# Sixteen blocks of a conditioned transformer layer: the attention's projection ahead of the last part of the MLP and of v

## The chip, the cores and the metric

The kernel runs on one core of one Trainium2 chip. A core has a matrix engine (TensorE, in the profile PE), a vector engine (DVE), a scalar engine (ACT), a general one (POOL) and a queue that issues DMAs (SP). Time is the device time of one execution in microseconds; of several executions the median is given.

## The reference

Everything is 32-bit floating point. For each of eight sequences of 1024 tokens of width 512, with a condition vector of its own, the layer computes:

```python
mod = jax.nn.silu(condition) @ Wada + bada
sh_a, sc_a, gt_a, sh_m, sc_m, gt_m = jnp.split(mod, 6, axis=1)
xm = layernorm(x) * (1.0 + sc_a) + sh_a
x = x + gt_a * attention(xm)           # 16 heads of 32, causal, softmax, then @ Wproj + bproj
xm = layernorm(x) * (1.0 + sc_m) + sh_m
h = jax.nn.gelu(xm @ W1 + b1)          # 512 -> 2048
x = x + gt_m * (h @ W2 + b2)           # 2048 -> 512
```

(the normalizations also have gains and offsets of their own; the modulation is a row for each sequence).

## The kernel before, in words

**Blocks and steps.** The 8 x 1024 tokens are cut into 16 blocks of 512 tokens, two a sequence: an even block is the first half of its sequence, an odd one the second half. A block goes through these steps, which are names in the plan: `at` (its normalized input is brought into the transposed layout and modulated), `q`, `k`, `v` (three projections), the attention in four groups of four heads, `proj` (the attention's output times Wproj, gated and added to the residual, and the second normalization set going), `mt` (the transposed, modulated input of the MLP; its 16 transposes are the matmuls of L735 that read `hat_m`), `u` 0 to 3 (the four quarters of the first MLP matrix) and `d` 0 to 3 (four parts of the second).

**Products in seven.** `q`, `k`, `v`, `u` and `d` use Strassen's scheme: seven products of half size in place of eight, on sums of weight pieces and of inputs that are kept. A `q`, `k`, `v` or `u` step is 7 products of 32 matmul instructions. `d` has 7 products of 128: two in `d0`, two in `d1`, one in `d2`, two in `d3`. In `d2` DVE combines its product into `u_d`, and three element-wise operations (POOL or DVE, as the planner finds them free) settle `v_d` into the residual `xr`. `proj` is 4 row tiles of 4 channel groups of 8 matmul instructions (N = 512), 128 in all. All of them are issued by one helper, line 202.

**Two streams on one engine.** TensorE runs two streams, interleaved: the attention (scores L1541, transposed weights L1620 and L1632, weighted values L1672, sums L1693, rows of maxima L1594), and the linear work, which is the list `plan`, sixteen windows in a row, one for each block w of the attention. Window w has the rest of the MLP of block w - 2, v of block w, `proj` and `mt` of block n = w - 1, k and q of block w + 1, and the first parts of the MLP of block n. A planner written in Python fixes the order of all instructions when the program is built, with estimated durations: the linear stream is paced so that window w ends when the attention of block w does (`stream["due"]` against `done_linear`). When linear work is behind, it goes first; when it is ahead, the attention goes first and the linear work fills its waits. Each engine then runs its own instructions in that order, and waits for others by semaphores where data or buffers ask for it.

**What orders the steps.** The main thread takes the steps of the plan strictly one after the other; `at`, `mt`, loads of the residual and stores are side threads, which run when what they ask for is there. A step asks by keys with times in `written`; a key at `NEVER` blocks until something sets it. `proj` of n asks for `("attended", n)`, set when the last quotient of its attention has been queued: after the sums of a group of heads, ACT copies them, DVE takes reciprocals (L1711) in four pieces, and POOL multiplies (L1736, `qT<-top,rec`). `mt` of n asks for `("v done", n + 1)`. The attention can't weigh values of block w before v of w is done (`close`, L1822): until then only linear work is issued. In an even block that is so from its first unit on; in an odd block the units over the first half of the sequence come before it. The steps of a turned `at` (blocks from 2 on): four DVE transposes, a write of 1 MB to DRAM (`held`), four reads back into the tile `hat`, four scalings. There is one `hat` tile, used by the inputs of `at` and then by those of `mt` (`hat_m`).

**Weights.** Pieces of 256 KB come through a ring of eight slots, in the order of the plan: a piece is fetched when the one eight before it has been released. `q`, `k`, `v` and `u` have seven pieces, `d0`, `d1` and `d3` eight, `d2` four, `proj` four, which are all released at its end. SP issues all of these DMAs, and the loads of inputs, the stores and the turns, in one order.

Of the kernel before, what the change touches and what calls it, by code (L numbers as in the profile page):

```python
# [22 lines left out]
def kernel(  # L23
# [42 lines left out]
    NC = D // P  # L66
# [28 lines left out]
    written, left = {}, {}  # L95
    shape = [None]
    pool_spans = []
    NEVER = float("inf")
# [13 lines left out]
    def note(engine, ns, reads=(), writes=(), port=False):  # L112
        start = max(now[engine], due(reads, writes))
        if port:
            start = max([start] + [b for a, b in pool_spans if a <= start < b])
        end = start + ns
        now[engine] = end
        if engine == "POOL":
            pool_spans.append((start, end))
            del pool_spans[:-16]  # L120
        for k in reads:
            left[k] = max(left.get(k, 0.0), end + SYNC)
        for k in writes:
            written[k] = end + SYNC
        return end
# [102 lines left out]
    def mlp_steps(n):  # L228
        return [("u", n, i) for i in range(NQ)] + [("d", n, part) for part in range(4)]
# [8 lines left out]
    late = []  # L238
    for w in range(1, NB):
        n = w - 1  # L240
        m = mlp_steps(n)
        even = blocks[n][1] == 0
        rows_a = [("rows", blocks[n][0], "a")] if even else []
        rows_m = [("rows", blocks[n][0], "m")] if even else []
        own = m[:1] + ([("load_xa", w + 2)] if w + 2 < NB else []) + m[1:3]
        own += [("norm_a", w + 2)] if w + 2 < NB else []
        if w == NB - 1:
            steps = late[:1] + rows_a + [("proj", n), ("mt", n)] + late[1:]
            steps += [("v", w)] + rows_m + own + m[3:5] + [("load_xr", w)] + m[5:6]
            late = m[6:]  # L250
        else:

            steps = late + [("v", w)] + rows_a + [("proj", n), ("mt", n), ("k", w + 1)]
            if w == 2:
                steps = late + [("v", w), ("k", w + 1)] + rows_a + [("proj", n), ("mt", n)]
            if w == 1:
                steps = rows_a + [("k", w + 1), ("proj", n), ("mt", n)]
            steps += [("q", w + 1)] + rows_m + own
            at = [("at", w + 2)] if w + 2 < NB else []
            if blocks[w][1] == 0:  # L260

                steps += m[3:5] + [("load_xr", w)]
                late = m[5:6] + at + m[6:]
            else:
                steps += m[3:5] + [("load_xr", w)] + m[5:6] + at
                late = m[6:]
        plan[w] = steps
    n = NB - 1
# [99 lines left out]
    at, r0 = [], 0  # L368
# [9 lines left out]
    def hat_tile(key):  # L378
        return tmp.tile([P, NTT, D], F32, tag="hat", name=f"hat_{key}", bufs=1)

    def load_x(n):
        b, h = blocks[n]
        rows = hat_tile(f"a{n}")
        for t in range(NTT):
            some = x[b, h * TB + t * P : h * TB + (t + 1) * P, :]
            if f"a{n}" in by_pe:
                nc.sync.dma_start(rows[:, t, :], some)
            else:
                nc.sync.dma_start(rows[ts(t, Q), :, :], some.rearrange("(t i) d -> i t d", i=Q))
        return rows  # L390
# [145 lines left out]
    act_jobs = []  # L536
# [43 lines left out]
    def normalize(tiles, key, sources):  # L580

        for t in range(NTT):
            written["hat", key, t] = NEVER
        mv = small.tile([P, NTT, 2], F32, tag="mv", name=f"mv_{key}")
        rstd = small.tile([P, NTT], F32, tag="rstd", name=f"rstd_{key}")
        offset = small.tile([P, NTT], F32, tag="offset", name=f"offset_{key}")

        def statistics(t):
            st = small.tile([P, nc.vector.BN_STATS_DIM], F32, tag="st", name=f"st_{key}_{t}")
            nc.vector.bn_stats(st, tiles[:, t, :])  # L590
            nc.vector.bn_aggr(mv[:, t, :], st)
            note("DVE", 850, [sources[t]], [("mv", key)])
            if t < NTT - 1:
                return
            if alone[0]:
                root()
                for i in range(NTT):
                    apply_tile(i)
                return
            power()  # L600
            for i in range(NTT):
                act_jobs.append((lambda i=i: apply_tile(i), [("rstd", key)]))

        def root():
            nc.scalar.activation(rstd, mv[:, :, 1], AF.Sqrt, bias=eps)
            note_act(300, "sqrt", [("mv", key)], [("rstd", key)])
            nc.vector.reciprocal(rstd, rstd)
            nc.vector.scalar_tensor_tensor(offset, mv[:, :, 0], -1.0, rstd, ALU.mult, ALU.mult)
            note("DVE", 360, [("rstd", key)], [("rstd", key)], port=True)

        def power():
            nc.gpsimd.tensor_scalar(rstd, mv[:, :, 1], EPS, None, ALU.add)
            nc.gpsimd.tensor_tensor(rstd, rstd, minus_half, ALU.pow)
            nc.gpsimd.tensor_scalar(offset, mv[:, :, 0], -1.0, None, ALU.mult)
            nc.gpsimd.tensor_tensor(offset, offset, rstd, ALU.mult)
            note("POOL", 1500, [("mv", key)], [("rstd", key)])

        to = [None]

        def apply_tile(t):  # L620
            if t == 0:
                hats[key] = to[0] = hat_tile(key) if key[0] == "m" else tiles
            xh, xt = to[0][:, t, :], tiles[:, t, :]
            reads, writes = [("rstd", key)], [("hat", key, t)]
            if (key == "a0" and t % 2) if alone[0] else sooner(reads, writes, 700, 800) == "DVE":
                nc.vector.tensor_scalar(
                    xh, xt, rstd[:, t : t + 1], offset[:, t : t + 1], ALU.mult, ALU.add
                )
                note("DVE", 700, reads, writes, port=True)
            else:  # L630
                nc.scalar.activation(
                    xh, xt, AF.Identity, bias=offset[:, t : t + 1], scale=rstd[:, t : t + 1]
                )
                note_act(800, None, reads, writes)

        for t in range(NTT):
            add_job(lambda t=t: statistics(t), [sources[t]], key[0] == "m")
# [54 lines left out]
    def modulated(key, gain, shift, b, guards):  # L692
# [22 lines left out]
        at = {t: (key, t) for t in part}  # L715
        if turned:
            yield from turn(key, got, xm)
        for c in range(NC):
            if turned:
                if c:  # L720
                    yield [("turned", key)], []
                source, out = ("turned", key), xm[:, c, :].rearrange("p (a x) -> p a x", x=P)
                values = got[:, :, ts(c, P)]
                if key[0] == "m":
                    out = xm[:, c, :].rearrange("p (t a x) -> p t a x", t=2, a=NTT)
                    values = values.rearrange("p a (t x) -> p t a x", t=2)
            else:
                if c:
                    yield [("hat", key, 0)], [BANK]
                bank = lin_bank()  # L730
                source, out, values = ("l", bank), xm[:, c, :], banks[bank]
                for t in range(NTT):
                    if t:
                        yield [("hat", key, t)], []
                    nc.tensor.transpose(banks[bank][:, ts(t, P)], got[:, t, ts(c, P)], ident)  # L735
                    note_pe(TR, "whole", [("hat", key, t)], [("l", bank)])
            writes = [at["B11"], at["T1"]] if c < 2 else [at["B21"], at["B22"]]
            if sooner([source], writes, 770, 780) == "DVE":
                nc.vector.tensor_scalar(
                    out, values, gain[:, c, b : b + 1], shift[:, c, b : b + 1],  # L740
                    ALU.mult, ALU.add,
                )
                note("DVE", 770, [source], writes, port=turned)
            else:
                nc.scalar.activation(  # L745
                    out, values, AF.Identity,
                    bias=shift[:, c, b : b + 1], scale=gain[:, c, b : b + 1],
                )
                note_act(780, None, [source], writes)
            if not turned:  # L750
                live[bank] = False
            if c == 1:
                nc.vector.tensor_tensor(part["T1"], part["T1"], part["B11"], ALU.subtract)
                note("DVE", 700, [at["B11"], at["T1"]], [at["T1"]], port=True)
# [1184 lines left out]
```

## Time and profile before

| | |
|---|---|
| median of 3 runs | 3546.27 us (3541.39 to 3548.4) |
| the profiled execution's own time | 3542.2 us |
| its span, first to last instruction | 3540.5 us |
| instructions | 120499 |
| mean granted TensorE clock | 0.998 |
| weights and data read, written in DRAM | 412.99 MB, 43.06 MB |

A row of a timeline has the start in us from the span's beginning, the length in us, the engine, the line, the operation, the tiles (output<-inputs) with partitions x elements, the number of instructions merged, and in brackets the engine's idle time before it with what ended it. `32*128` is the size of a TensorE tile in rows and columns. A row of a stage gives its bounds and length, the busy time (and instructions) of each engine in it, the granted TensorE clock, the share of the DMA engines and GB/s.

### The profile page before, as it was taken

The numbers are of one execution on the slowest core, as the hardware profiler recorded it, in microseconds if no ns is written. First come the engines' busy times: TensorE is split into PE (matmuls) and PEld (weight loads), VectorE is DVE, ScalarE is ACT, GpSimd is POOL, SyncE is SP. The second block draws the span as 40 slices with busy tenths as digits, with TensorE's granted clock in tenths as the row PEclk, the third lists the DMA queues.
The fourth block names the chain that finished last, engine by engine and source line by source line (L and its number), as shares of the span: only waits on it lengthen the run. The fifth ranks groups of instructions, "written<-read, shape, count | busy, mean of one in ns | idle before, by whom it ended". The sixth has DMA issues, their size and how long they took to land.

```text
span 3540.5 us, 120499 instructions
## 1 busy us (share of the span) xinstructions
PE 3482.5 (98%) x54621; PEld 1738.0 (49%) x54621; DVE 2174.2 (61%) x2383; ACT 1190.1 (34%) x1237; POOL 2074.9 (59%) x2249
## 2 busy tenths in 40 slices
PE   8999999999999999999999999999999999999999
PEld 4444445445554555545554454544545445454445
DVE  5776675564756557565675656656566556655563
ACT  2334323352333513235232342323423234232521
POOL 2667836666376664666546675366762667526660
PEclk9999999999999999999999999999999999999999
DMA  6753434335443354524445334443344533443334
GB/s 198 245 163 103 137 117 140 111 111 156 117 148 103 110 160 117 168 85 126 142 118 159 103 115 141 124 149 107 118 132 127 156 106 119 135 126 124 100 110 140
DMA packets 319555, 465.96 MB, mean 132 GB/s; under 512 B 26300, under 2 KB 176636, under 8 KB 316996
## 3 DMA queue, kind: packets, MB, share of 16 engines
q1 hardware_dynamic: 318928, 458.22, 42.9%
q8 instruction: 430, 7.05, 0.8%
q14 instruction: 81, 0.66, 0.1%
q10 hardware_dynamic: 116, 0.03, 0.0%
HBM read 412.99 MB, written 43.06 MB: 129 GB/s over the span
## 4 chain that ended last, share of the span: by engine, by line
PE 88%; DMA 4%; DVE 3%; POOL 2%; issue 1%; ACT 1%; SPq 0%; ACTq 0%; DVEq 0%; POOLq 0%
PE bank L202 61%; PE sc L1541 8%; PE po L1672 7%; PE st L1632 7%; PE st L1620 3%; DMA w<-in_L_cond_Wproj_dram 2%; PE bank L1693 2%; PE bank L735 1%; DVE mx L1556 1%; POOL pT L1762 1%; DMA w<-in_L_cond_Wada_dram 1%; PE bank L1594 0%; POOL hT L161 0%; POOL xr L161 0%; DVE sc L1553 0%
## 5 line engine op out<-in xcount | busy, mean ns | idle before, releaser
L1762 POOL TENSOR_TENSOR pT<-pT,pT 128x256 f32<-128x256 f32 (+3 forms) x1254 | 1207.2, 998 | 347.9 <-PE po L1672 181.4
L1644 ACT ACTIVATE pT<-st 128x2048 f32<-128x2048 f32 x288 | 541.0, 1879 | 1000.5 <-PE st L1632 883.3
L202 PE MATMUL bank<-w,hT 128*32 128x256 f32 x14336 | 812.3, 380 | 1.1 <-ACT rec L1702 0.9
L1556 DVE TENSOR_REDUCE mx<-sc 128x4 f32<-128x2048 f32 (+3 forms) x384 | 666.0, 1755 | 197.7 <-PE sc L1541 191.6
L202 PEld LDWEIGHTS bank<-w,hT 128*32 128x32 f32 x14336 | 450.4, 110 | 369.2 <-issue 81.4
L202 PE MATMUL bank<-xm_m,w 128*32 128x256 f32 x8192 | 499.6, 381 | 0.0
L202 PE MATMUL bank<-t_m,w 128*32 128x256 f32 x6144 | 381.2, 380 | 0.0
L1649 POOL TENSOR_SCALAR_AFFINE_SELECT pT<-pT 128x512 f32<-128x512 f32 x256 | 168.8, 677 | 346.6 <-ACT pT L1644 344.2
L202 PEld LDWEIGHTS bank<-xm_m,w 128*32 128x32 f32 x8192 | 255.7, 110 | 224.7 <-issue 62.4
L1553 DVE TENSOR_TENSOR sc<-sc,mask 128x1024 f32<-128x1024 f32 (+1 forms) x160 | 162.9, 1018 | 319.7 <-PE sc L1541 242.5
L1541 PE MATMUL sc<-kT,qT 32*128 32x512 f32 (+3 forms) x3072 | 329.1, 520 | 1.8 <-DVE mx L1556 1.1
L1672 PE MATMUL po<-pT,v 128*32 128x512 f32 (+3 forms) x3048 | 302.9, 492 | 2.0 <-POOL pT L1649 2.0
L1632 PE MATMUL st<-qT,kT 32*128 32x512 f32 (+3 forms) x3072 | 301.0, 487 | 0.0
L202 PEld LDWEIGHTS bank<-t_m,w 128*32 128x32 f32 x6144 | 190.0, 110 | 173.3 <-issue 48.5
L202 PE MATMUL bank<-xm_a,w 128*32 128x256 f32 x3968 | 249.3, 382 | 0.0
L202 PE MATMUL bank<-w,qT 128*32 128x512 f32 x2048 | 238.2, 594 | 8.7 <-DMA w<-in_L_cond_Wproj_dram 7.2
L1711 DVE RECIPROCAL rec<-rec 128x128 f32<-128x128 f32 x256 | 225.7, 920 | 31.5 <-ACT rec L1702 31.5
L1541 PEld LDWEIGHTS sc<-kT,qT 32*128 32x128 f32 x3072 | 129.3, 183 | 179.3 <-issue 73.0
L193 DVE TENSOR_TENSOR hT<-bank,u_u 128x512 f32<-128x512 f32 x192 | 129.9, 687 | 114.1 <-PE bank L202 107.4
L202 PE MATMUL bank<-t_a,w 128*32 128x256 f32 x2944 | 188.4, 382 | 0.4 <-ACT xm_m L745 0.4
L1069 ACT ACTIVATE hT<-hT,cols 128x512 f32<-128x512 f32 x256 | 164.4, 711 | 35.5 <-DVE hT L193 35.0
L202 PEld LDWEIGHTS bank<-xm_a,w 128*32 128x32 f32 x3968 | 122.7, 110 | 105.5 <-issue 32.6
(216 smaller groups left out, 3384.6 us busy)
## 6 DMA issues: line engine op xcount, KB each, us to landing
w<-in_L_cond_W_dram SPq DMA_DIRECT2D x384, 256.0 KB
w<-kept_up_S SPq DMA_DIRECT2D x256, 256.0 KB
w<-kept_down_S SPq DMA_DIRECT2D x256, 256.0 KB
w<-kept_qkv_S SPq DMA_DIRECT2D x180, 256.0 KB
w<-in_L_cond_Wqkv_dram SPq DMA_DIRECT2D x147, 256.0 KB
hat_a<-in_x_dram SPq DMA_DIRECT2D x64, 256.0 KB
xr<-in_x_dram SPq DMA_DIRECT2D x32, 512.0 KB
w<-in_L_cond_Wproj_dram SPq DMA_DIRECT2D x64, 256.0 KB
```

Of the source, the lines that this page charges most:

```text
L193: nc.vector.tensor_tensor(out, src, other, op)
L202: nc.tensor.matmul(ps[r, :], columns, rhs, start=start, stop=stop, skip_group_check=True)
L1069: nc.scalar.activation(hT[:, i, :], hT[:, i, :], AF.Gelu, bias=cols[:, O_B1 + f : O_B1 + f + 1])
L1541: nc.tensor.matmul(sc[:, j, c0 : c0 + w], qTs[n][r, gg, ts(qt, P)], keys_of(n, kh)[r, gg, :w], start=True, stop=True, skip_group_check=True,)
L1553: nc.vector.tensor_tensor(place, place, shape_of.to_broadcast(place.shape), ALU.add)
L1556: nc.vector.tensor_reduce(maxima[n, gg][:, kh, qt, :], sc[:, :, c0 : c0 + w], axis=AX.X, op=ALU.max)
L1632: nc.tensor.matmul(st[:, j, c0 : c0 + w], kT[r, gg, ts(k % NTT, P)], qT[r, gg, TB - w :], start=False, stop=True, skip_group_check=True,)
L1644: nc.scalar.activation(pT[:, :, :used], st[:, :, :used], AF.Exp, scale=scale)
L1649: nc.gpsimd.affine_select(diagonal, diagonal, pattern=[[0, HPG], [1, P]], compare_op=ALU.is_ge, fill=0.0, base=0, channel_multiplier=-1,)
L1672: nc.tensor.matmul(po[r, TB - w :], v[:, k % NTT, g * P + j * hd : g * P + (j + 1) * hd], pT[:, j, c0 : c0 + w], start=(k == 0), stop=last ...
L1711: nc.vector.reciprocal(some, some)
L1762: nc.gpsimd.tensor_tensor(into, into, pT[:, j, c0 : c0 + w], ALU.add)
```

## The change

In windows 3 to 14 the order of the linear steps changes. Windows 1, 2 and 15 keep theirs.

- Even windows, before: `d2 d3 v proj mt k`; after: `d2 proj mt d3 v k`.
- Odd windows, before: `d1 at d2 d3 v proj mt k`; after: `at d1 d2 proj mt d3 v k`. Here `at` is that of block w + 1, and d1 to d3 are those of block w - 2.
- In odd windows the loads of the gates' row for the new sequence (`rows_a`) go with `proj`.
- A new key, `"hat free"`: set to `NEVER` when the input of an `at` is loaded into the tile `hat`, and to 0 when the last scaling of that `at` has been issued. The scalings that write `hat_m` wait for it in the planner's list. It adds no instruction.

No computation is added, removed or changed in form; the same weight pieces are loaded in the new order of the plan.

```diff
-            steps = late + [("v", w)] + rows_a + [("proj", n), ("mt", n), ("k", w + 1)]
+            steps = late[:-1] + rows_a + [("proj", n), ("mt", n)] + late[-1:] + [("v", w), ("k", w + 1)]
             if w == 2:
                 steps = late + [("v", w), ("k", w + 1)] + rows_a + [("proj", n), ("mt", n)]
...
                 steps += m[3:5] + [("load_xr", w)]
-                late = m[5:6] + at + m[6:]
+                late = at + m[5:]
...
     def load_x(n):
         b, h = blocks[n]
         rows = hat_tile(f"a{n}")
+        written["hat free"] = NEVER
...
         for t in range(NTT):
             written["hat", key, t] = NEVER
+        free = ["hat free"] if key[0] == "m" else []
...
             power()
             for i in range(NTT):
-                act_jobs.append((lambda i=i: apply_tile(i), [("rstd", key)]))
+                act_jobs.append((lambda i=i: apply_tile(i), [("rstd", key), *free]))
...
             if not turned:
                 live[bank] = False
+            if c == NC - 1 and key[0] == "a":
+                written["hat free"] = 0.0
```

## The prediction

> **What bounds the kernel now.** First the head of the page and its table of engines.
>
> ```profile
> span 3540.5 us, 120499 instructions
> PE 3482.5 (98%) x54621; PEld 1738.0 (49%) x54621; DVE 2174.2 (61%) x2383; ACT 1190.1 (34%) x1237; POOL 2074.9 (59%) x2249
> ```
>
> TensorE works in 98% of the span: 58.0 us of idling are all that a new order can win back, while each microsecond for which it makes PE wait is a microsecond of the kernel. So the second view is who PE waited for, and I cut it to 580:3000 us, the blocks that the change touches (columns: total, times, longest).
>
> ```profile
> PE bank L202 <- DMA w<-in_L_cond_Wproj_dram: 7.2, 9, 1.5
> PE st L1620 <- DVE mx L1556: 3.8, 3, 1.6
> ```
>
> The longest of these, 7.2 us, is one wait: the projection for its weights. Third, the timeline of PE where block 7 of the attention hands over to block 8 (an even block: it needs a new v at once).
>
> ```profile
> 1685.32 1.04 PE L1693 MATMUL bank<-pT,ones 128*32 128x512 f32 x8
> ...
> 1696.53 3.23 PE L202 MATMUL bank<-w,hT 128*32 128x256 f32 x56
> 1699.58 0.41 PE L1594 MATMUL bank<-ident_b,mcols 128*32 128x128 bf16 x16
> 1699.80 13.56 PE L202 MATMUL bank<-w,hT 128*32 128x256 f32 x248
> 1723.54 1.90 PE L202 MATMUL bank<-w,qT 128*32 128x512 f32 x16
> 1726.20 1.92 PE L202 MATMUL bank<-w,qT 128*32 128x512 f32 x16 [0.75 <-DMA w<-in_L_cond_Wproj_dram]
> 1731.38 1.04 PE L1672 MATMUL po<-pT,v 128*32 128x512 f32 x8
> ```
>
> At 1685.32 the sums of the last head group of block 7 are made (L1693); from 1699.80 on PE runs the MLP's last part, v and the start of the projection in one piece, because the attention can't go on (next `po` at 1731.38) before v of block 8 is done. This piece, which I call the hold, is where all moved steps lie.
>
> **The change part by part.**
>
> *The wait for Wproj goes.* The queue of weight loads (SP) shows why it exists.
>
> ```profile
> 1712.18 0.42 SPq L1118 DMA_DIRECT2D out_dram<-xr  x1
> 1712.70 3.60 SPq L685 DMA_DIRECT2D hat_a<-held_a  x4
> 1716.39 0.85 SPq L342 DMA_DIRECT2D w<-in_L_cond_Wproj_dram  x2
> 1717.34 0.39 SPq L1118 DMA_DIRECT2D out_dram<-xr  x1
> 1717.82 1.48 SPq L342 DMA_DIRECT2D w<-in_L_cond_Wproj_dram  x2
> ```
>
> Ring slots come free in order of use, eight ahead. Today the four Wproj pieces follow the pieces of v, are issued behind stores and the turn's four reads, 7 us ahead of their use, and all four are needed in the first row tile. Afterwards they follow d2's four pieces, so their slots come free in d1's second product, and all of d2 (128 matmuls, 7.0 us by the row of 248 in 13.56 us) lies between. Gain 7.2 us, all there is; the other end is 0 (another load is late instead). Next to be late would be d3's last four pieces, whose slots the projection frees only at its end; they have d3's first product, again 128 matmuls and 7.0 us, before they are needed, and the four stores and reads above are then no longer ahead of them: I take 0. The stores of d3 move behind the projection on SP, v's and k's loads stand behind them as today. In odd windows the turn's write and four reads go ahead of d1's loads; nothing but the ring's lead of eight pieces covers them, and that is what covers them now.
>
> *A new wait: the projection for the attention's last quotient.* In odd windows the projection now stands behind d1 and d2, 384 matmuls or 21 us, and the quotient is done as they begin (first row below, window 9). In even windows only d2 is ahead of it. When d2 ends, DVE makes `u_d` of its product; when the last head group is divided by its sum, POOL writes `qT` (L1736), and the projection multiplies with that. Both, behind that first row, for the even windows 4, 6, 8, 10, 12, 14:
>
> ```profile
> 1877.27 1.27 POOL L1736 TENSOR_TENSOR qT<-top,rec 128x512 f32<-128x512 f32 x1
> 830.76 1.29 POOL L1736 TENSOR_TENSOR qT<-top,rec 128x512 f32<-128x512 f32 x1
> 832.64 0.69 DVE L193 TENSOR_TENSOR u_d<-bank,p_d 128x512 f32<-128x512 f32 x1 [1.43 <-PE bank L202]
> 1266.30 0.69 DVE L193 TENSOR_TENSOR u_d<-bank,p_d 128x512 f32<-128x512 f32 x1 [1.13 <-PE bank L202]
> 1271.04 1.73 POOL L1736 TENSOR_TENSOR qT<-top,rec 128x512 f32<-128x512 f32 x1
> 1699.40 0.69 DVE L193 TENSOR_TENSOR u_d<-bank,p_d 128x512 f32<-128x512 f32 x1 [0.42 <-PE bank L202]
> 1704.14 1.73 POOL L1736 TENSOR_TENSOR qT<-top,rec 128x512 f32<-128x512 f32 x1
> 2131.80 0.69 DVE L193 TENSOR_TENSOR u_d<-bank,p_d 128x512 f32<-128x512 f32 x1 [0.38 <-PE bank L202]
> 2137.13 1.28 POOL L1736 TENSOR_TENSOR qT<-top,rec 128x512 f32<-128x512 f32 x1
> 2566.12 0.69 DVE L193 TENSOR_TENSOR u_d<-bank,p_d 128x512 f32<-128x512 f32 x1 [0.74 <-PE bank L202]
> 2573.02 1.29 POOL L1736 TENSOR_TENSOR qT<-top,rec 128x512 f32<-128x512 f32 x1
> 3000.99 0.68 DVE L193 TENSOR_TENSOR u_d<-bank,p_d 128x512 f32<-128x512 f32 x1
> 3006.92 1.27 POOL L1736 TENSOR_TENSOR qT<-top,rec 128x512 f32<-128x512 f32 x1
> 1737.34 4.50 PE L202 MATMUL bank<-w,qT 128*32 128x512 f32 x40
> ```
>
> From d2's end to the end of the quotient: in window 4 nothing (832.05 against 832.64), then 6.5, 6.5, 6.6, 8.2 and 7.2 us. POOL settles d2's result before it gets to the quotient, so the distance hangs on d2's end itself. Today d3 fills it; the attention can't, for it is held. Of this time the first row tile can use 24 matmuls on the three groups that are ready, at 4.50/40 = 0.11 us each 2.6 us, and the maxima's rows (L1594) 0.2 us. What remains: 3.7 + 3.7 + 3.8 + 5.4 + 4.4 = 21.0 us of idle PE. Ends: 0 (the quotient is queued earlier) and 36 (5 × 7.2, if the first matmul waits as well). I take 21: rows for each of the five say so. While PE stands, d3's and v's matmuls are queued behind the projection, and the attention waits for v.
>
> *The clock after such a wait.* The rows of stages have the granted clock (PEclk) behind the busy times.
>
> ```profile
> 218.40:221.84 3.44, 1.03 (x16) 0.39 (x12) 2.29 (x1) 0.00 (x0) 3.21 (x5) 1.00 0.24 76
> 221.84:225.25 3.41, 3.41 (x20) 0.42 (x12) 2.87 (x3) 1.49 (x1) 3.33 (x5) 0.50 0.02 5
> 3395.00:3399.00 4.00, 1.96 (x32) 0.70 (x28) 1.17 (x3) 0.00 (x0) 3.92 (x3) 1.00 0.38 130
> ```
>
> After a stretch with 2.4 us of idling the clock was 0.50 for 3.4 us; after 2.0 us of idling around 3397 it stayed. A wait of 3.7 us and more should trip it in nearly all cases: half of 3.41 us, 1.7 us, times 5, or 8 us. Ends 0 and 17 (two such stretches each). The Trainium skill, "TensorE: Matmul & The Clock Gate", Part 1: The HAM clock gate, puts the fall to half rate after at least one idle window of about 3.4 us. By that rule a wait of 3.7 us would hardly ever hold a whole window, the 8 would be near 1 and the sum 7 us lower. The trace differs (1.03 us of matmuls in that window, and it fell), and the measurement decides.
>
> *The transposes of `mt` go in fewer pieces.* Today the normalized rows come one at a time while q runs, and the transposes slip in singly:
>
> ```profile
> 1781.87 1.05 PE L202 MATMUL bank<-t_a,w 128*32 128x256 f32 x16
> 1782.85 0.33 PE L735 MATMUL bank<-ident,hat_m 128*128 128x128 f32 x1
> 1783.11 1.07 PE L202 MATMUL bank<-t_a,w 128*32 128x256 f32 x16
> 3248.58 1.09 PE L735 MATMUL bank<-ident,hat_m 128*128 128x128 f32 x8
> ```
>
> One alone held PE for 0.26 us (1782.85 to 1783.11), one of eight for 1.09/8 = 0.14, and the 16 matmuls before it took 0.98 us to it where 16 take 13.56 × 16/248 = 0.87: a piece costs some 0.12 + 0.11 = 0.23 us beyond its work. Counted in the timeline, eleven of the windows 3 to 14 have five or six pieces and window 12 has three; window 15, which has the new order today, has two (one of them shown). Afterwards rows are ready when v is done (statistics and scaling pass under d3 and v), so I take three pieces: 2.5 × 0.23 × 11 = 6 us gained; ends 0 and 9 (two pieces).
>
> *The rest at nothing.* The projection's own 128 matmuls, 14 us, move inside the hold and lengthen it; the attention makes this up under k, q and u afterwards:
>
> ```profile
> 1506.90:1600.00 93.10, 54.69 (x836) 25.30 (x840) 1.00 0.32 92
> 1600.00:1685.30 85.30, 59.46 (x1044) 32.00 (x1033) 1.00 0.38 119
> ```
>
> These are L202 alone in block 7: 59% of PE after the hold, while the attention catches up, 70% from 1600 on. The missing 14 us × 30% = 4.2 us of attention come back at 11% in about 40 us of those 85. Without that cover the odd block would end late and the wait above grow with it. The marker "hat free" is no instruction; it holds back four scalings on ACT, for which nobody waits until v is done. DVE's first multiplication of the projection may wait for POOL's three operations on d2's result: three banks cover 3.5 us each.
>
> The sum against the profiled execution, 3542.2 us: + 21 + 8 - 7 - 6 = + 16, 3558. That execution lies 4.1 us under the median of the runs shown, 3546.27, so the forecast for the median is 3562.
>
> **The rivals.**
>
> *The quotient is early (faster).* If the planner queues the last reciprocal and the quotient before d2's product ends, as in window 4 (done 0.6 us before `u_d`), no even window waits: - 7 - 6, 3533. It decides once the quotient ends less than 2.8 us after d2. For it: window 4, and that a blocked main thread makes the planner flush its queued jobs. Against it: in the other five, POOL's settling stands ahead of the quotient, and that is queued as d2 ends.
>
> *The clock holds.* With PE's clock at 1.00 after the waits, which the row at 3395 speaks for and the one at 221.84 against, and the waits as above: + 21 - 7 - 6 = + 8, 3554, at the edge of what can be told from no change. This is what the Trainium skill's rule in "TensorE: Matmul & The Clock Gate" would give.
>
> *The attention doesn't catch up (slower still).* If the hold's 14 us are not made up by the end of an odd block, PE reaches the projection earlier against the quotient; 3 us more in each of five windows are 15 us: 3577. For it: PE is full already. Against it: half the 85 us suffice.
>
> **How the numbers follow.** Forecast 0.50 (own range 3554 to 3573); early quotient 0.23; clock holds 0.12; no catching up 0.15. About 0.2%, 7 us, is what a measurement of this kernel can tell from no change. Slower: the forecast's 0.49, 0.15 and 0.03 of the clock's, 0.67. The same: 0.09 + 0.01 + 0.01 = 0.11. Faster: 0.22. The range from 3530 to 3580 leaves out the lower half of the faster case and the upper part of the last, under 2 in 10.
>
> **What would show it.** Right: in the changed profile the wait for Wproj is gone between 580 and 3000 us; five new waits of L202 for POOL `qT` L1736, of 3 to 6 us, at the starts of even windows, each followed by 3.4 us at clock 0.50; PE's matmuls on `hat_m` in two to four pieces, right after v. Wrong: no wait for `qT`, or waits on attention tiles (`st`, `po`) in their place; PE's busy time changed by more than the half clock and the pieces explain; Wproj's wait replaced by one for d3's last weights.

## The result, and the profile after

| | before | after |
|---|---|---|
| median of 6 runs each | 3547.09 us | 3560.86 us |
| range | 3541.39 to 3549.82 | 3556.19 to 3563.13 |
| span of the profiled execution | 3540.5 us | 3559.7 us |
| mean granted TensorE clock | 0.998 | 0.993 |

The ratio is 1.0039, with a 95% interval of 1.0026 to 1.0052: 0.4% slower. The medians lie 13.8 us apart, the two profiled executions 19.2 us, because the one profiled before took 4.9 us less than its kernel's median. The accounts of single terms below go by the profiled executions.

The head of the page and the table of engines after:

```profile
span 3559.7 us, 120551 instructions
PE 3484.8 (98%) x54621; PEld 1737.8 (49%) x54621; DVE 2171.7 (61%) x2371; ACT 1187.1 (33%) x1231; POOL 2095.3 (59%) x2267
```

The same 54621 matmuls take 2.3 us more of busy time, and PE's idling went from 58.0 to 74.9 us. Whom PE waited for, over the whole kernel (total, times, longest; lines behind 400 stand up to four higher than before):

```profile
PE bank L202 <- POOL qT L1740: 20.6, 5, 4.5
PE bank L422 <- ACT cond_act L416: 6.6, 1, 6.6
PE bank L202 <- DVE y L193: 5.5, 1, 5.5
PE bank L202 <- DMA w<-in_L_cond_Wada_dram: 5.2, 6, 3.8
PE st L1624 <- DVE mx L1560: 4.4, 4, 2.4
```

Wproj's line is gone (its 7.2 us before were not one wait but nine, of 0.2 to 1.5 us each, in windows of both parities). A line for the quotient (`qT`) with five waits has come, and one that the prediction did not name: 5.5 us for `y`, the product of the projection with its gate, on DVE. The timeline of PE at the start of window 8, which answers to the hold shown before:

```profile
1693.02 2.80 PE L202 MATMUL bank<-w,hT 128*32 128x256 f32 x48
1695.63 0.41 PE L1598 MATMUL bank<-ident_b,mcols 128*32 128x128 bf16 x16
1695.85 2.76 PE L202 MATMUL bank<-w,qT 128*32 128x512 f32 x24
1702.36 14.04 PE L202 MATMUL bank<-w,qT 128*32 128x512 f32 x104 [3.75 <-POOL qT L1740]
1716.22 13.99 PE L202 MATMUL bank<-w,hT 128*32 128x256 f32 x256
...
1742.22 1.09 PE L737 MATMUL bank<-ident,hat_m 128*128 128x128 f32 x8
1743.24 1.07 PE L1676 MATMUL po<-pT,v 128*32 128x512 f32 x8
...
1746.44 1.09 PE L737 MATMUL bank<-ident,hat_m 128*128 128x128 f32 x8
```

The first row tile of the projection makes its 24 matmuls on the three groups that are ready, then PE stands for 3.75 us; and the 16 transposes come in two pieces of eight right behind v, where window 8 had five before. Rows of stages, with the granted clock third from the end, for the stretches behind the five waits (and, last, behind the wait for `y`):

```profile
1267.47:1270.88 3.41, 3.41 (x20) 0.87 (x16) 0.76 (x2) 0.00 (x0) 3.41 (x3) 0.50 0.37 116
1700.96:1707.79 6.83, 5.43 (x28) 1.39 (x32) 2.58 (x3) 0.00 (x0) 5.46 (x4) 0.50 0.71 224
2141.28:2144.70 3.42, 3.42 (x20) 0.87 (x16) 0.69 (x1) 0.00 (x0) 3.27 (x3) 0.50 0.40 97
2578.19:2581.60 3.41, 3.41 (x20) 0.87 (x16) 1.14 (x2) 0.00 (x0) 3.41 (x3) 0.50 0.75 308
3011.68:3018.50 6.82, 4.56 (x24) 1.19 (x28) 1.39 (x3) 0.00 (x0) 2.21 (x3) 0.50 0.39 156
3028.75:3035.57 6.82, 5.93 (x28) 1.39 (x32) 3.77 (x5) 0.00 (x0) 6.66 (x6) 0.50 0.27 77
```

The clock was 0.50 behind every one of them. Half of PE's busy time there is lost: the 104 matmuls above, which start in such a stretch, took 14.04 us, where at the pace of the 128 in 13.92 us that a later row shows they would take 11.3. That makes (3.41 + 5.43 + 3.42 + 3.41 + 4.56)/2 = 10.1 us behind the quotient, 3.0 us behind `y`.

**The account.** Idle PE: + 20.6 (quotient) + 5.5 (`y`) - 7.2 (Wproj) = + 18.9, measured 74.9 - 58.0 = + 16.9; the other - 2 us are the sum of small changes, the largest of them in the attention's wait of `st` for `mx` (7.4 us before, 4.4 after). Busy PE: + 13.1 (half clock; its stretches before 230 us and after 3400 us cost 6.2 us before and 6.4 after) - 9.8 (pieces of transposes, at a price that the last group of experiments measures) = + 3.3, measured + 2.3. A difference of 3 us in all stays unassigned.

### The profile page after: what moved, and what is told of

The parts are those of the page before. It is cut to its first block, busy times and chain, and to the rows that moved or that the text cites. A ratio compares the mean times of both kernels' runs of the same rounds, so it can differ in the third digit from the quotient of the medians.

```text
span 3559.7 us, 120551 instructions
## 1 busy us (share of the span) xinstructions
PE 3484.8 (98%) x54621; PEld 1737.8 (49%) x54621; DVE 2171.7 (61%) x2371; ACT 1187.1 (33%) x1231; POOL 2095.3 (59%) x2267
## 5 line engine op out<-in xcount | busy, mean ns | idle before, releaser
L202 PE MATMUL bank<-w,qT 128*32 128x512 f32 x2048 | 240.3, 621 | 28.1 <-POOL qT L1740 20.6
L1579 POOL CAST mcols<-mx 128x16 bf16<-128x16 f32 x56 | 15.6, 278 | 280.7 <-DVE mx L1574 145.8
```

Of the source, the lines that this page charges most:

```text
L202: nc.tensor.matmul(ps[r, :], columns, rhs, start=start, stop=stop, skip_group_check=True)
L1579: engine.tensor_copy(high, m)
```

## The experiments

Theory: in the even windows the projection comes ahead of the quotient, which costs the wait and the half clock behind it; the rest of the change is a gain. Rivals stand with each run. All are compared with the kernel before on the same chip.

**One parity at a time.** The new order in the odd windows alone:

```diff
+            if w % 2 == 0:
+                steps = late + [("v", w)] + rows_a + [("proj", n), ("mt", n), ("k", w + 1)]
```

> The new order in the odd windows only; the even windows keep d2 d3 v proj mt k. Theory (the loss is the even windows' wait for the attention's last quotient, and the half clock after it): no wait of the projection for qT and no half clock after 300 us; Wproj's waits of the odd windows gone (about 4 of 7.2 us) and the transposes of six blocks in two pieces each (about 7 us): 11 us faster than before, ratio 0.997. Rival (the longer hold itself costs, since the attention can't make it up): half of the measured loss of 14 us, ratio 1.002.

3533.78 us, ratio 0.9970 (0.9958 to 0.9981). No wait for `qT`, no half clock in the blocks concerned; of Wproj's waits six were left, 4.4 us together, all in even windows.

And in the even windows alone:

```diff
+            if w % 2:
+                steps = late + [("v", w)] + rows_a + [("proj", n), ("mt", n), ("k", w + 1)]
...
-                late = at + m[5:]
+                late = m[5:6] + at + m[6:]
```

> The new order in the even windows only; the odd windows keep d1 at d2 d3 v proj mt k. Theory: the five waits for qT (about 21 us), the half clock after them (10 to 13 us) and the later wait for DVE in window 14 (5.5 us) all stay, and only half of the gains is left (3 us of Wproj, 7 us of transposes): 25 to 30 us slower than before, ratio 1.007 to 1.009. Rival (longer hold): half of the loss, ratio 1.002.

3571.63 us, ratio 1.0077 (1.0063 to 1.0091). The loss lies in the even windows: they alone cost 26 us, the odd ones alone gain 12, and the sum is the + 14 of the whole change. Whom PE waited for in this run:

```profile
PE bank L202 <- POOL qT L1742: 20.6, 5, 4.5
PE bank L202 <- DVE y L193: 5.6, 1, 5.6
PE bank L202 <- DMA w<-in_L_cond_Wproj_dram: 5.5, 7, 1.1
```

**A cover for the quotient.** In the even windows the projection goes behind d3, still ahead of v:

```diff
+            if w % 2 == 0:
+                steps = late + rows_a + [("proj", n), ("mt", n), ("v", w), ("k", w + 1)]
```

> As the changed kernel, but in the even windows the projection stands behind d3 and ahead of v (d2 d3 proj mt v k). Theory: d3's 14 us cover the quotient, which ends at most 8.2 us after d2: no wait for qT, no half clock, and all gains stay (7 us of Wproj, 14 us of transposes): 21 us faster than before, ratio 0.994. Rival (longer hold): the hold is as long as in the changed kernel, so its loss stays, ratio 1.004.

3523.59 us, ratio 0.9943 (0.9931 to 0.9956). The hold is as long as in the changed kernel, and the kernel is 22 us faster than before: the rival falls, and no cost of the longer hold shows. The expected 14 us of transposes did not come, though: blocks 2 to 13 have 30 pieces here against 63 before, 8 us at the price measured last. With Wproj's 7.2 us that is 15.5 of the 18.4 us between the profiled executions; the rest is not assigned. The same in the odd windows too:

```diff
-            steps = late[:-1] + rows_a + [("proj", n), ("mt", n)] + late[-1:] + [("v", w), ("k", w + 1)]
+            steps = late + rows_a + [("proj", n), ("mt", n), ("v", w), ("k", w + 1)]
```

> The projection between d3 and v in the odd windows too. Theory (what counts is that the projection stands where weights and quotient are ready, and ahead of v so that mt's rows are): as with the even windows alone, 3524 us, ratio 0.994. Rival (the early place in the odd windows gave gains of its own): slower than that by 3 us or more.

3522.79 us, ratio 0.9937 (0.9924 to 0.9951): the same within the intervals, with a simpler plan. This is the version that beats both. Its hold in window 8, from PE's timeline, has no idle time at all:

```profile
1688.54 13.56 PE L202 MATMUL bank<-w,hT 128*32 128x256 f32 x248
1701.92 13.92 PE L202 MATMUL bank<-w,qT 128*32 128x512 f32 x128
1715.66 1.91 PE L202 MATMUL bank<-w,xm_a 128*32 128x256 f32 x32
```

**Why the quotient is late, and what the clock costs.** First the changed kernel with the last quotient of odd blocks on DVE:

```diff
-            if n == NB - 1 and g == NC - 2:
+            if (n == NB - 1 and g == NC - 2) or (n % 2 and g == NC - 1):
                 nc.vector.tensor_tensor(qTs[n][:, g, :], top, rec, ALU.mult)
```

> The changed kernel, with the last quotient of each odd block multiplied on DVE right behind the last reciprocal, in place of POOL behind the three operations that settle d2. Theory (POOL's queue makes the quotient late): it ends some 2.4 us after d2 in windows 6, 8 and 10, which the 24 free matmuls cover, and 4.8 us after in 12 and 14: waits for it fall from 20.6 us to about 4, the half clock to at most two stretches; some 27 us faster than the changed kernel, ratio to before about 0.997. Rival (the reciprocals on DVE are late, not POOL): waits of 15 us and more stay, ratio 1.003.

3535.79 us, ratio 0.9971 (0.9963 to 0.9980). In window 8 of the changed kernel the last reciprocal was done at 1697.43, and POOL came to the quotient at 1700.59, behind its three operations on d2's result (rows of both engines' timelines):

```profile
1696.49 0.94 DVE L1715 RECIPROCAL rec<-rec 128x128 f32<-128x128 f32 x1
1696.65 1.28 POOL L161 TENSOR_TENSOR v_d<-v_d,u_d 128x512 f32<-128x512 f32 x1 [0.24 <-DMA w<-kept_down_S]
1698.01 1.28 POOL L161 TENSOR_TENSOR v_d<-v_d,row_gm 128x512 f32<-128x512 f32 x1
1699.37 1.26 POOL L161 TENSOR_TENSOR xr<-xr,v_d 128x512 f32<-128x512 f32 x1
1700.59 1.71 POOL L1740 TENSOR_TENSOR qT<-top,rec 128x512 f32<-128x512 f32 x1
```

In this run DVE had it done 2.6 us after `u_d` began (with POOL it was 6.4):

```profile
1693.93 0.69 DVE L193 TENSOR_TENSOR u_d<-bank,p_d 128x512 f32<-128x512 f32 x1 [0.42 <-PE bank L202]
1695.59 0.94 DVE L1737 TENSOR_TENSOR qT<-top,rec 128x512 f32<-128x512 f32 x1
```

The waits fell from 20.6 to 6.9 us, with two stretches of half clock behind the two long ones, 3.6 and 2.6 us in windows 12 and 14. So the place behind POOL's three operations makes most of the lateness: the move took 13.7 us of waits away (of the 3.8 us that it saved in window 8, 0.8 are DVE's shorter multiplication). Most of the rest is the rival's, since in windows 12 and 14 DVE itself makes all four reciprocals only after `u_d`.

Then the changed kernel with PE kept at work in the wait, by products that are thrown away:

```diff
-    def accumulate(pairs, reads=(), close=True):
+    def accumulate(pairs, reads=(), close=True, starts=(0,)):
...
-            matmul(banks[bank], lhsT, rhs, i == 0, close and i == len(pairs) - 1, reads, bank)
+            matmul(banks[bank], lhsT, rhs, i in starts, close and i == len(pairs) - 1, reads, bank)
...
+                twice = n % 2 and n > 4 and t == 0
                 bank = yield from accumulate(
-                    [(attT[:, c, ts(t, P)], piece(at[c])) for c in range(NC)], [("att", n)]
+                    [(attT[:, c, ts(t, P)], piece(at[c])) for c in [0, 1, 2] * twice + list(range(NC))],
+                    [("att", n)], True, (0, 3) if twice else (0,),
                 )
```

> The changed kernel, where the first row tile of the projection in windows 6, 8, 10, 12 and 14 makes its first three products twice (24 matmuls more, 2.6 us, thrown away by the second start), so that TensorE works through most of the wait for the quotient without ending it sooner. Theory (the half clock after the wait is a cost of its own): the idle part of the waits falls from 20.6 to about 8 us, the clock stays at 1.00 after them, and the kernel is 8 to 10 us faster although it does more: ratio to before 1.001 to 1.002. Rival (the clock costs nothing beside the wait): no faster than the changed kernel, ratio 1.004.

3539.48 us, ratio 0.9986 (0.9977 to 0.9995): some 19 us faster than the changed kernel by the two ratios, with 13 us more of matmuls, and twice the gain that was expected. The idle rest of the waits was 4.3 us in three, none over 1.4, and the clock stayed at 1.00 from the first blocks to 3400 us. The wait for `y` had gone as well, which the expectation had not reckoned with: in window 14 two products of the gate now stood ahead of the scaling on DVE that the next group is about. Between the profiled executions, 25.7 us apart, PE's idling fell from 74.9 to 52.1 us, by 16.3 at the quotient and 5.5 at `y`. Its busy time fell from 3484.8 to 3481.9 us although 13.0 us of matmuls had been added, so 15.9 us of it had gone: 10.1 and 3.0 are the half clock behind the quotient and `y`, and 2.0 are less of it before 230 us and after 3400 us. The rival falls.

**The wait for `y`.** The timeline of DVE in window 14 of the changed kernel:

```profile
3010.65 2.42 DVE L673 STREAM_TRANSPOSE xm_a<-hat_a 128x512 f32<-128x512 f32 x4
3025.32 0.55 DVE L741 TENSOR_SCALAR xm_a<-hat_a,gaina,shifta 128x512 f32<-128x512 f32 x1 [12.25 <-DMA hat_a<-held_a]
3028.90 1.28 DVE L193 TENSOR_TENSOR y<-bank,row_ga 128x512 f32<-128x512 f32 x2
```

DVE stood for 12.25 us on a scaling whose input was still on its way back from DRAM, and the projection's first two gate products, in its queue behind that, could not empty their banks; all three were full and PE stood. The test alters only the planner's estimate of the way:

```diff
-    HOLDING = 8000
+    HOLDING = 12000
```

> The changed kernel, with the planner's estimate for each way of the turn through DRAM raised from 8 to 12 us, which only alters where the scalings of the turned input are queued. Theory (in window 14 the projection's first product of the gate stood in DVE's queue behind a scaling that waited for the turn's read-back, and three full banks then stopped PE for 5.5 us): that wait and the half clock after it go, 5 to 9 us faster than the changed kernel, ratio to before 1.001 to 1.002; the five waits for qT stay at 20 us. Rival (DVE waited for the projection itself): the wait of 5.5 us stays.

3551.99 us, ratio 1.0021 (1.0013 to 1.0030), some 6 us less than the changed kernel by the two ratios; the wait for `y` and its half clock were gone, the five for `qT` stood at 20.6 us. DVE now makes all four products of the gate ahead of the scaling, which finds its input there (the first of them, and the scaling):

```profile
3012.34 0.68 DVE L193 TENSOR_TENSOR y<-bank,row_ga 128x512 f32<-128x512 f32 x1
3026.58 0.55 DVE L741 TENSOR_SCALAR xm_a<-hat_a,gaina,shifta 128x512 f32<-128x512 f32 x1
```

In the run with the quotient on DVE all four products came ahead of the scaling too, without this edit, and the wait for `y` is missing there as well. The order in DVE's queue was the cause.

**The price of a piece of transposes.** A first try, in the kernel before, started `mt` behind q:

```diff
-            steps = late + [("v", w)] + rows_a + [("proj", n), ("mt", n), ("k", w + 1)]
+            steps = late + [("v", w)] + rows_a + [("proj", n), ("k", w + 1)]
...
-            steps += [("q", w + 1)] + rows_m + own
+            steps += [("q", w + 1)] + [("mt", n)] * (w > 2) + rows_m + own
```

> The kernel before, with mt started behind q in place of ahead of k (windows 3 to 14), so that all normalized rows are ready when its transposes start. Theory (a piece of transposes slipped between column matmuls costs some 0.25 us beyond its work, and the changed kernel's 64 pieces down to 24 gave about 12 us): two to four pieces a block in place of five or six, 6 to 12 us faster than before, ratio 0.997 to 0.998, with Wproj's 7 us of waits unchanged, if the first MLP product does not then wait for its input. Rival (pieces cost nothing; the time came from elsewhere): ratio 1.000.

3551.27 us, ratio 1.0020 (1.0011 to 1.0029), slower and not faster: even blocks still had four or five pieces, and other waits came, of scores and weights for the maxima on DVE above all (16.8 us in all, 8.5 before). It does not tell the price. The second try spreads the transposes on purpose, in the version with the projection behind d3 everywhere:

```diff
                 for t in range(NTT):
-                    if t:
-                        yield [("hat", key, t)], []
+                    if t or key[0] == "m" and 1 < int(key[1:]) < 14 and c:
+                        written["apart"] = now["PE"] + 100 if key[0] == "m" and 1 < int(key[1:]) < 14 else 0.0
+                        yield [("hat", key, t), "apart"], []
```

> The kernel with the projection between d3 and v in all of windows 3 to 14, with the transposes of mt of blocks 2 to 13 spread on purpose: one at a time between other matmuls, some 190 pieces in place of some 30, nothing else changed. Theory (a piece costs TensorE about 0.25 us beyond its work): some 160 pieces x 0.25 = 40 us slower than that kernel's 3523, so 3563, ratio to before 1.005. Rival (pieces cost nothing by themselves): 3523, ratio 0.994.

3562.15 us, ratio 1.0049 (1.0035 to 1.0062). The tables of engines, first of the version with whole pieces, then of this one:

```profile
PE 3472.9 (99%) x54621; PEld 1739.4 (49%) x54621; DVE 2183.9 (62%) x2384; ACT 1186.7 (34%) x1230; POOL 2081.3 (59%) x2255
```

```profile
PE 3517.2 (99%) x54621; PEld 1735.6 (49%) x54621; DVE 2176.0 (61%) x2380; ACT 1185.4 (33%) x1229; POOL 2087.1 (59%) x2260
```

The same 54621 matmuls take 44.3 us more. Of these 3.7 us are the clock: PE's work in stretches at 0.50 is 12.8 us in the one and 20.1 in the other. Counted in the timelines, blocks 2 to 13 have 30 pieces in the one and 192 in the other: (44.3 - 3.7)/162 = 0.25 us a piece, and the rival falls. The kernel before has 63 such pieces and the changed kernel 24: 39 × 0.25 = 9.8 us gained. The Trainium skill, "TensorEngine Tiling (Array Packing)", Key Properties, says that changing the tiling mode drains TensorE, and gives no time. The runs fit that, though they show only the price, 0.25 us for the way from tiles of 128*32 to 128*128 and back.

## Why the prediction was right, point by point

- **The wait for Wproj goes, - 7**: right, 7.2 to 0, and the load named as next to be late (d3's last pieces) caused no wait.
- **The new wait, + 21**: right. Five waits in windows 6 to 14, none in 4, 20.6 us together; the single sizes 4.0, 3.8, 4.3, 4.1 and 4.5 against 3.7, 3.7, 3.8, 5.4 and 4.4. That three of four groups could be used first holds (24 matmuls stand ahead of the wait), and that the quotient hangs on d2's end and POOL's settling holds: taking it off POOL took 13.7 of the 20.6 us away.
- **The half clock, + 8**: right in kind, somewhat short: 10.1 us, since two of the five stretches lasted 6.8 us and not 3.4. The Trainium skill's rule ("TensorE: Matmul & The Clock Gate", Part 1) asks for a whole idle window. Here the clock fell behind all five waits, though PE had worked 0.43 to 1.20 us in the 3.41 us ahead of each fall; the measurement decides.
- **The transposes, - 6**: the mechanism was right, the size not. Two pieces a block, not three, and 0.25 us a piece, not 0.23: 9.8 us, just beyond the far end that was given, 9.
- **The rest at nothing**: this step failed in one place. The prediction had DVE's first gate product wait for POOL alone, covered by three banks; in window 14 it waited behind a scaling for a DMA, and 5.5 us of idling and 3.0 us of half clock came of it. In the list of what is queued behind a waiting instruction, the turn's scalings on DVE were missing. That the attention makes up the longer hold fits: two versions with as long a hold are 22 us faster than before.

By the measured sizes: + 20.6 + 10.1 - 7.2 - 9.8 = + 13.7 for the terms that were forecast, + 8.5 for the one that was not, - 3 elsewhere: + 19.2 in the profiled execution, where + 16 was predicted. So the time came out right partly by luck: the transposes' larger gain (4 us) and the small changes elsewhere (3 us) stood against the missed wait (8.5 us).

## What to carry to other kernels

When a step is moved ahead on an engine that is always busy, look up when its last input is ready relative to its new place, not its old one: 14 us of cover moved to the wrong side of it turned a gain of 22 us into a loss of 14. Put the step behind the piece of work that just outlasts the wait. And where tile shapes alternate on TensorE, let work of the odd shape wait until it can run in one piece.

## What the runs showed of the hardware that was not expected

- The clock changes on a fixed beat of 3.413 us, and its falls go by how long PE works in one beat, not by how long a gap is. In every trace the starts of the stretches at 0.50 lie whole multiples of 3.413 us apart (from 1267.47 to 1700.96 are 127). The rows of stages below are beats of the changed kernel, with PE's busy time first behind the length. The first, second and fourth end with a fall behind the quotient; the third is the beat ahead of the fourth, in which the same wait began.

```profile
1264.06:1267.47 3.41, 0.43 (x4) 0.16 (x8) 3.41 (x3) 0.00 (x0) 3.41 (x3) 1.00 0.65 269
2137.87:2141.28 3.41, 0.81 (x8) 0.29 (x12) 3.09 (x3) 0.00 (x0) 3.41 (x3) 1.00 0.74 303
2571.36:2574.77 3.41, 1.52 (x16) 0.26 (x8) 3.38 (x6) 0.67 (x2) 2.97 (x3) 1.00 0.19 68
2574.77:2578.19 3.42, 1.20 (x12) 0.42 (x16) 3.42 (x7) 0.00 (x0) 2.52 (x3) 1.00 0.00 0
```

After 0.43, 0.81 and 1.20 us of work the clock fell; after 1.52 us it stayed for one more beat. In all eleven traces, from 35 us on and up to 8 us before the end, it fell after every beat with less than 1.39 us of work and after none with more than 1.76; between these, both happened. This sorts gaps of much the same length. Gaps of 2.64 us (quotient on DVE, window 14) and 2.41 us (before the change, at 221 us) left 1.0 us of work in a beat, and the clock fell; gaps of 2.38 and 2.39 us (`mt` behind q, at 929 and 1364 us) and of 2.27 us (projection behind d3, at 2321 us) left 1.9, 1.7 and 1.95 us, and it stayed. All this is read from traces of runs that were made for other ends; none was made to test it.

- The half clock lasted one beat or two, 3.4 us or 6.8. In the changed kernel it lasted two where the wait reached into the first of them, so that PE worked only 2.02 us of it (window 8), 1.15 (window 14) and 2.52 (behind `y`). It lasted one where PE worked all of the first, 3.41 us (windows 6, 10 and 12). In the other traces a first beat with less than 2.9 us of work was always followed by a second, and one with more than 3.35 us never.
